# Four graph layers on one core: a written order for the first pass of the last layer, and its adjacency kept as fp8

## The chip, the cores and the metric

The kernel runs on one core of one Trainium2 chip. The time is the device time of one execution in microseconds (us). A core has the engines PE (TensorE: matmuls and transposes into PSUM), ACT (ScalarE), DVE (VectorE), POOL (GpSimd) and SP (SyncE, used here only to issue DMAs). Each engine runs its own list of instructions in order and waits at an instruction whose inputs, or whose output buffer, are not there yet. ACT and POOL issue DMAs as well, from the same list as their computing.

## The reference

Sixteen graphs (B) of 1024 nodes (N) with 128 features (D). `adj` is a 0/1 matrix for each graph. Four layers follow one another, each as `x = layernorm(x + layer(x))`:

- layer 0: attention masked by `adj`
- layer 1: for each node the maximum over its neighbours of `relu(p_i + q_j + b)`
- layer 2: sum over neighbours, then a two-layer perceptron
- layer 3: first a pruned adjacency, made row by row ("dilation": every so many neighbours of a row are removed, together with the mirrored entry, so that later rows see what earlier rows removed), then three SAGE steps with a batch norm over all graphs after each:

```python
def _sage(x, adj, Wr, Wx, b, mf):
    deg = jnp.clip(jnp.sum(adj, axis=-1, keepdims=True), 1.0, None)
    agg = jnp.einsum('bij,bjd->bid', adj, x) / deg
    out = agg @ Wr + x @ Wx + b
    nrm = jnp.maximum(jnp.linalg.norm(out, axis=-1, keepdims=True), NORM_EPS)
    return out / nrm * mf[..., None]

adj_d = _dilate(adj, mask)
h1 = _bn(jax.nn.relu(_sage(x, adj_d, Wr1, Wx1, b1, mf)), g1, be1)
h2 = _bn(jax.nn.relu(_sage(h1, adj_d, Wr2, Wx2, b2, mf)), g2, be2)
h3 = _bn(jax.nn.relu(_sage(h2, adj_d, Wr3, Wx3, b3, mf)), g3, be3)
xc = jnp.concatenate([h1, h2, h3], axis=-1) * mf[..., None]
return (xc @ Wl + bl) * mf[..., None]
```

A batch norm needs all sixteen graphs, so layer 3 falls into passes over the graphs. The dilation needs only `adj`, not the features.

## The kernel before, in words

**Main loop (`layers_012`).** `slot(s, last)` (L853) is one step of layer 1's maximum; 86 slots make a graph (`NP`), 1376 the loop. Beside each slot a planner lets streams advance: `scores` and `attend` of the next graph (layer 0), `rest` of the graph before (layer 2), and `dilation()`, which handles 32 rows (R) of all graphs at a time and writes what is removed to `removed` in DRAM (`removed<-gone`, L611). The planner's costs and due times fix the order, and the loop stands inside `tc.manual_schedule`, which keeps PE, ACT, DVE and POOL in the order of the program. `load_columns(at)` (L749) loads chunk `at` (120 rows, 9 chunks to a graph) of the transposed adjacency `adjT` from fp32 into the fp8 tile `AT`, by a POOL DMA that casts. `AT` has four buffers.

**After the loop.** The last graph's `rest` (L402: relu of the maximum, layer norm, sum over neighbours `pa`, perceptron `pp` and `py`, layer norm) is written out next, and then `first_edges()` (L1124), which loads layer 3's weights through ACT's DMA queue (`weight`, L112) and calls `edges(0)`, `settle(0)` and `edges(1)`. From the end of the loop on, the order on each engine is the scheduler's.

**Edges.** `edges(b)` (L967) makes the pruned adjacency of graph b. `load_edges` (L957) brings in `gone_all` (the removals) and `near` (the transposed adjacency, once more from fp32), both by casting POOL DMAs. For each of 16 half rows of chunks, PE adds the removals and their transpose in PSUM (`pgone`, L973 and L975: five matmuls) and DVE clears the edge in `near` (L977). `near` is stored as `kept`. Then 16 matmuls count the degrees (`pdeg`, L984), ACT copies them, and a DMA to DRAM and one back turn the row of 1024 into 8 rows of 128 (`degree`, `deg_t`). `settle` (L991) takes min, max and reciprocal on DVE and stores `there` and `share` to DRAM; `load_share` (L999) reads `share` back to all 128 partitions.

**First pass (L1145 to L1158), for each graph.** `expanded` (L1004) turns `near` into eight fp32 chunks `m` on ACT. `convolve` (L1011) splits the features into `high` (ACT) and `low` (DVE), sums over neighbours in 32 matmuls (`pagg`, L1021) and multiplies by `share` (`u`, L1024). `sage` (L1027) makes `po` from the features and from `u` (L1032, L1035), `o` on ACT, transposes to `rows`, squares (ACT), sums (DVE), takes the power -1/2 on POOL (L1051) and writes the rows `r_rows` on DVE (L1055). `pass_on` (L1116) transposes back (`phid`, L1063), keeps statistics, stores `hidden`, and runs `convolve` again on the new rows for the second pass (`around`). At the end of graph b the program calls `edges(b + 2)`.

**The rest.** `second(b)` (L1160) and `pass_on` make the second pass, `second` and `columns` the third, `summed` and a layer norm the output. They use the same helpers.

Of the kernel before, what the change touches and what calls it, by code (L numbers as in the profile page):

```python
# [48 lines left out]
R, G = 32, 4  # L49
K, Q = N // R, B // G  # L50
# [23 lines left out]
def tile_graph_layers(ctx: ExitStack, tc, a, out):  # L74
# [6 lines left out]
    small = ctx.enter_context(tc.tile_pool(name="small", bufs=3))  # L81
    psum = None
# [14 lines left out]
    penalty = consts.tile([P, P], BF, name="penalty")  # L97
# [7 lines left out]
    lit = consts.tile([CH, PC, P], F8, name="lit")  # L105
    nc.gpsimd.dma_start(out=lit, in_=a["lit"])
    less = consts.tile([P, P], F32R, name="less")
    nc.vector.tensor_scalar_mul(less, ident, -1.0)
    one_less = consts.tile([P, 1], F32, name="one_less")
    nc.sync.dma_start(out=one_less, in_=a["one_less"])  # L110

    def weight(name, shape=(P, P), how=None, pool=consts):  # L112
        t = pool.tile(list(shape), F32, name="w_" + name)
        src = a[name] if how is None else a[name].rearrange(how[0], **how[1])
        nc.scalar.dma_start(out=t, in_=src)
        return t

    def column(name, n=1, pool=consts):
        return weight(name, (P, n), ("(c p) -> p c", {"p": P}), pool)

    def row(name, pool=consts):
        return weight(name, (1, P), ("(o f) -> o f", {"o": 1}), pool)
# [5 lines left out]
    Wd = consts.tile([P, P], F32, name="Wd")  # L128
# [4 lines left out]
    eps1 = consts.tile([P, 1], F32, name="eps1")  # L133
# [3 lines left out]
    def in_three(v, name):  # L137

        p = bank("p3")
        nc.tensor.matmul(p[:, :P], ones[0:1, :], v, start=True, stop=True)  # L140
        left = temp.tile([3, P], F32, name="left_b")
        nc.vector.tensor_copy(left, p[:3, :P])
        e = consts.tile([3, P], BF, name=name)
        nc.vector.memset(e, 0.0)
        for i in range(3):
            part = temp.tile([3, P], BF, name="part_b")
            nc.vector.tensor_copy(part, left)
            if i < 2:
                nc.vector.tensor_sub(left, left, part)
            nc.vector.scalar_tensor_tensor(e, part, ident[:3, i:i + 1], e, op0=ALU.mult, op1=ALU.add)  # L150
        return e
# [8 lines left out]
    half_mask = consts.tile([B, N], F32, name="half_mask")  # L160
# [7 lines left out]
    half_rows = consts.tile([P, K, Q], F32, name="half_rows")  # L168
# [6 lines left out]
    of_graph = consts.tile([P, G], F32, name="of_graph")  # L175
    nc.vector.tensor_reduce(of_graph, ident.rearrange("p (g r) -> p g r", g=G), axis=mybir.AxisListType.X, op=ALU.add)

    above = consts.tile([P, Q, R], BF, name="above")
    nc.vector.memset(above, 1.0)
    running = consts.tile([P, Q, R], BF, name="running")  # L180
# [5 lines left out]
    of_row = consts.tile([P, R], F32, name="of_row")  # L186
# [6 lines left out]
    removed_T = dram.tile([K, P, Q, N], BF, name="removed_T")  # L193

# [43 lines left out]
    def layers_012():  # L238
# [510 lines left out]
        def load_columns(at):  # L749
            b, c = divmod(at, T + 1)  # L750
            if b < B:
                rows = min(CH, N - c * CH)
                t = AT[at] = apool.tile([CH, N], F8, name="AT", bufs=4)
                if rows < CH:
                    nc.gpsimd.memset(t, 0.0)
                nc.gpsimd.dma_start(out=t[:rows], in_=adjT[b, c * CH:c * CH + rows])
# [96 lines left out]
        def slot(s, last):  # L853
# [11 lines left out]
            if s >= 0 and g % PC == 0:  # L865
                load_columns(b * (T + 1) + g // PC + 2)
# [62 lines left out]
        assert not streams, streams  # L929
        last = rest(B - 1)  # L930
        for _ in range(15):
            next(last)
        for _ in dilate:
            pass
        right.close()
        for _ in last:
            pass
        psums.close()
        psum = ctx.enter_context(tc.tile_pool(name="psum", bufs=2, space=PSUM))
        first_edges()  # L940


# [14 lines left out]
    def load_edges(b):  # L957
        gone = ep.tile([P, T, N], F8, name="gone_all")
        q, g = divmod(b, G)
        rows = removed[:, g * R:(g + 1) * R, q, :].rearrange("(c k) r i -> k r c i", c=T)  # L960
        for k in range(P // R):
            nc.gpsimd.dma_start(out=gone[k * R:(k + 1) * R], in_=rows[k])
        near = ep.tile([P, T, N], F8, name="near", bufs=2)
        nc.gpsimd.dma_start(out=near, in_=adjT[b].rearrange("(c p) i -> p c i", p=P))
        return gone, near

    def edges(b):  # L967

        gone, near = load_edges(b)
        for c in range(T):  # L970
            for h, s in enumerate(halves):
                p = bank("pgone")
                nc.tensor.matmul(p, ident_b, gone[:, c, s], start=True, stop=False)  # L973
                for t in range(4):
                    nc.tensor.matmul(p[:, t * P:(t + 1) * P], gone[:, 4 * h + t, c * P:(c + 1) * P], ident_b,  # L975
                                     start=False, stop=(t == 3))
                nc.vector.tensor_tensor(near[:, c, s], near[:, c, s], p, op=ALU.is_gt, saturate=False)  # L977
        nc.sync.dma_start(out=kept[b], in_=near)

        deg = ep.tile([1, N], F32, name="deg")  # L980
        for s in halves:
            p = bank("pdeg")
            for c in range(T):
                nc.tensor.matmul(p, ones_b, near[:, c, s], start=(c == 0), stop=(c == T - 1))  # L984
            nc.scalar.copy(deg[:, s], p[0:1, :])
        nc.sync.dma_start(out=degree[b], in_=deg)
        d = ep.tile([T, P], F32, name="deg_t", bufs=2)
        nc.sync.dma_start(out=d, in_=degree[b].rearrange("(t i) -> t i", t=T))
        return near, d

    def settle(b, d):  # L991
# [12 lines left out]
    def expanded(near):  # L1004
        m = []
        for c in range(T):
            m.append(sb.tile([P, N], F32R, name="m", bufs=10))
            nc.scalar.copy(m[c], near[:, c, :])  # L1008
        return m

    def convolve(src, m, part):  # L1011

        high = sb.tile([P, T, D], F32R, name="high3")
        nc.scalar.copy(high, src)
        low = sb.tile([P, T, D], F32R, name="low3")
        nc.vector.tensor_sub(low, src, high.bitcast(F32))
        pa = wide("pagg")
        for c in range(T):
            for k, piece in enumerate((high, low)):
                for s in halves:  # L1020
                    nc.tensor.matmul(pa[:, s], piece[:, c, :], m[c][:, s],  # L1021
                                     start=(c == 0 and k == 0), stop=(c == T - 1 and k == 1))
        u = sb.tile([P, N], F32, name="u")
        nc.vector.tensor_mul(u, pa, part)  # L1024
        return u

    def sage(b, u, h, z, weights):  # L1027
# [3 lines left out]
        for s in halves:  # L1031
            nc.tensor.matmul(po[:, s], wx, h[:, s], start=True, stop=False)  # L1032
            if extra is not None:
                nc.tensor.matmul(po[:, s], extra, z[:, s], start=False, stop=False)
            nc.tensor.matmul(po[:, s], wr, u[:, s], start=False, stop=True)  # L1035
        o = sb.tile([P, N], F32, name="o", tag="sq", bufs=2)
        nc.scalar.activation(o, po, AF.Identity, bias=bias)
# [3 lines left out]
        for h in range(2):  # L1041
# [3 lines left out]
            sq = sb.tile([P, 4, D], F32, name="sq_rows")  # L1045
# [6 lines left out]
        nc.gpsimd.tensor_mul(n, n, nm[:, :, b])  # L1052
        for h in range(2):
# [4 lines left out]

    def columns(b, r, stats):
        for h in range(2):  # L1060
            p = bank("phid")
            for t in range(4):
                nc.tensor.transpose(p[:, t * P:(t + 1) * P], r[:, 4 * h + t, :], ident)  # L1063
            nc.scalar.copy(R3[b][:, halves[h]], p)
            nc.vector.bn_stats(out=stats[:, 2 * b + h, :], in_=p)
# [55 lines left out]
    ep, ahead = None, {}  # L1121
    Wr = Wx = bs = gs = bes = Wl = bl = None

    def first_edges():  # L1124
        nonlocal ep, Wr, Wx, bs, gs, bes, Wl, bl
        ep = ctx.enter_context(tc.tile_pool(name="ep", bufs=1, side="right"))
        Wr, Wx, bs, gs, bes = ([f(f"L3_gnn_{w}{l}", pool=ep) for l in (1, 2, 3)] for w, f in (
            ("Wr", weight), ("Wx", weight), ("b", column), ("g", column), ("be", column)))
        Wl = weight("L3_gnn_Wl", (P, 3, P), ("(c p) o -> p c o", {"p": P}), ep)
        bl = column("L3_gnn_bl", pool=ep)  # L1130
        ahead[0] = edges(0)
        settle(0, ahead[0][1])
        ahead[1] = edges(1)

    with ExitStack() as es:
# [6 lines left out]
    nc.vector.tensor_copy(pl, bl)  # L1142
    stats = sb.tile([P, 2 * B, 6], F32, name="stats", bufs=2)
    weights = Wr[0], Wx[0], bs[0], None
    for b in range(B):  # L1145
        x0 = sb.tile([P, T, D], F32, name="h", bufs=2)
        nc.sync.dma_start(out=x0, in_=x3[b])
        part = load_share(b)
        m = expanded(ahead[b][0])
        transposed(R3[b], x0)  # L1150
        r = sage(b, convolve(x0, m, part), R3[b], None, weights)
        if b + 1 < B:
            start = len(nc.cur_bb.bb.instructions)
            settle(b + 1, ahead[b + 1][1])
            behind(nc.cur_bb.bb.instructions[start - 1], start)
        pass_on(b, 0, r, m, part, stats)
        if b + 2 < B:
            ahead[b + 2] = edges(b + 2)  # L1158

    def second(b):  # L1160
# [4 lines left out]
        return sage(b, u, R3[b], z, weights)  # L1165

    weights = batchnorm(0, stats)
    stats = sb.tile([P, 2 * B, 6], F32, name="stats", bufs=2)
    r = second(0)
    for b in range(B):  # L1170
        near = ep.tile([P, T, N], F8, name="near", bufs=2)
        nc.sync.dma_start(out=near, in_=kept[b])
        part = load_share(b)
        following = second(b + 1) if b + 1 < B else None
        pass_on(b, 1, r, expanded(near), part, stats)
# [11 lines left out]
    def summed(b):  # L1187
        hs = []
        for l in range(2):
            r = sb.tile([P, N], F32, name="m", bufs=10)  # L1190
# [11 lines left out]
    for b in range(B):  # L1202
        following = summed(b + 1) if b + 1 < B else None
        xb = sb.tile([P, T, D], F32, name="xb", tag="m", bufs=10)
# [41 lines left out]
```

## Time and profile before

| | |
|---|---|
| median of 3 runs | 6267.28 us (6261.64 to 6274.73) |
| profiled execution | 6289.34 us, its span 6287.6 us |
| mean granted PE clock | 0.951 |
| busy over the span | PE 5624.7 us (89%), DVE 4878.2 (78%), ACT 3981.7 (63%), POOL 3635.9 (58%) |
| main loop, last DVE step | 5002.43 us |
| first pass, PE busy from 5120 to 5780 us | 532.69 of 660 us |
| second pass, PE busy from 5824 to 6040 us | 213.37 of 216 us |
| third pass, PE busy from 6045 to 6166 us | 103.64 of 121 us |
| output, PE busy from 6168 us to the end | 98.12 of 119.6 us |

The page's second part shows each engine in 40 slices of 157 us. A digit is the busy share in tenths; `PEclk` is the clock that the chip granted to PE. An answer by windows gives the same for stretches that one chooses. The chain of waits follows the work that ended last back through what released each step. A busy PE is not PE at its peak: matmuls are pipelined, and the distance from start to start says more than the length of one.

### The profile page before, as it was taken

The numbers are of one execution on the slowest core, as the hardware profiler recorded it, in microseconds if no ns is written. First come the engines' busy times: TensorE is split into PE (matmuls) and PEld (weight loads), VectorE is DVE, ScalarE is ACT, GpSimd is POOL, SyncE is SP. The second block draws the span as 40 slices with busy tenths as digits, with TensorE's granted clock in tenths as the row PEclk, the third lists the DMA queues.
The fourth block names the chain that finished last, engine by engine and source line by source line (L and its number), as shares of the span: only waits on it lengthen the run. The fifth ranks groups of instructions, "written<-read, shape, count | busy, mean of one in ns | idle before, by whom it ended". The sixth has DMA issues, their size and how long they took to land.

```text
span 6287.6 us, 92692 instructions
## 1 busy us (share of the span) xinstructions
PE 5624.7 (89%) x30144; PEld 3091.0 (49%) x30250; DVE 4878.2 (78%) x7402; ACT 3981.7 (63%) x7266; POOL 3635.9 (58%) x11895
## 2 busy tenths in 40 slices
PE   6989999999899989899999999999998678787998
PEld 4545454545454545454444545444543345555654
DVE  3888889898989888888888989888898644444455
ACT  3667676676767676767676767676665533333855
POOL 2676767677767776767776767677776411110113
PEclk8999999999999999999999999999999888898999
DMA  5121212121212121212121212121210246563645
GB/s 39 11 32 21 36 22 36 21 36 22 35 21 36 23 35 21 35 21 35 21 36 21 39 22 35 28 29 29 29 27 11 40 90 128 105 122 106 212 162 187
DMA packets 478410, 317.44 MB, mean 50 GB/s; under 512 B 301162, under 2 KB 429668, under 8 KB 473828
## 3 DMA queue, kind: packets, MB, share of 16 engines
q0 software_dynamic: 105648, 84.20, 15.6%
q1 hardware_dynamic: 367600, 226.13, 12.3%
q8 instruction: 237, 3.88, 0.3%
q10 hardware_dynamic: 4676, 1.19, 0.1%
q14 instruction: 249, 2.04, 0.1%
HBM read 412.71 MB, written 117.18 MB: 84 GB/s over the span
## 4 chain that ended last, share of the span: by engine, by line
PE 31%; DVE 11%; ACT 5%; POOL 4%; issue 2%; DMA 1%; ACTq 0%; SPq 0%; DVEq 0%; POOLq 0%
PE pg L835 7%; PE pagg L1021 6%; DVE best L900 5%; PE pm L804 3%; PE pa L435 1%; PE pav L393 1%; PE pp L296 1%; PE po L1035 1%; ACT hot L805 1%; PE pdeg L984 1%; POOL length L1051 1%; DVE sub L482 1%; PE prank L595 1%; PE psc L345 1%; PE pgone L973 1%
## 5 line engine op out<-in xcount | busy, mean ns | idle before, releaser
L900 DVE TENSOR_TENSOR best<-best,pg 128x1024 f32<-128x1024 f32 x2720 | 3263.5, 1215 | 496.1 <-PE pg L835 484.9
L805 ACT ACTIVATE hot<-pm,one_less 128x512 fp32r<-128x512 f32 x2752 | 1887.2, 689 | 746.7 <-PE pm L804 739.0
L835 PE MATMUL pg<-hot,high 64*128 64x512 f32 x5504 | 1411.2, 509 | 196.0 <-DVE best L900 166.2
L835 PE MATMUL pg<-hot,low 64*128 64x512 f32 x5504 | 1119.7, 404 | 0.0
L804 PE MATMUL pm<-AT,lit 120*128 120x512 fp8e4 x2752 | 1091.2, 397 | 4.0 <-ACT low L826 3.0
L835 PEld LDWEIGHTS pg<-hot,high 64*128 64x128 f32 x5504 | 525.4, 188 | 954.6 <-DVE best L900 440.0
L665 POOL TENSOR_SCALAR sc<-low_counts,half_mask,rest 16x1 f32<-16x1 f32 x992 | 355.9, 359 | 398.5 <-DVE rest L651 287.8
L835 PEld LDWEIGHTS pg<-hot,low 64*128 64x128 f32 x5504 | 540.6, 193 | 0.0
L804 PEld LDWEIGHTS <-lit 120*128 120x128 fp8e4 x2752 | 270.3, 98 | 395.4 <-issue 319.4
L670 POOL TENSOR_SCALAR sc<-sc 16x1 f32<-16x1 f32 x992 | 399.6, 403 | 105.1
L826 ACT CAST low<-pt 128x256 fp32r<-128x256 f32 x688 | 256.1, 372 | 256.6 <-PE pt L824 255.3
L1051 POOL TENSOR_TENSOR length<-length,mhalf 128x8 f32<-128x8 f32 x48 | 78.9, 1644 | 570.1 <-DVE length L1050 570.1
L667 POOL TENSOR_SCALAR sc<-sc 16x1 f32<-16x1 f32 x992 | 322.3, 325 | 107.7
L672 POOL TENSOR_SCALAR hit<-V,sc 16x31 bf16<-16x31 bf16 (+30 forms) x992 | 361.3, 364 | 0.0
L673 POOL TENSOR_SCALAR last_rank<-V,sc 16x31 f32<-16x31 bf16 (+30 forms) x992 | 346.0, 349 | 0.0
L824 PE MATMUL pt<-high,less 128*128 128x256 f32 x688 | 278.8, 405 | 67.7 <-ACT high L819 61.1
L482 DVE TENSOR_TENSOR sub<-sub,q 128x24 f32<-128x24 f32 (+11 forms) x768 | 308.0, 402 | 24.8 <-ACT q L300 10.4
L816 PE MATMUL pt<-ident,sub 128*128 128x128 f32 x1376 | 278.4, 284 | 54.1 <-ACT hot L805 51.8
L1008 ACT CAST m<-near 128x1024 fp32r<-128x1024 fp8e4 x256 | 253.3, 1044 | 113.1 <-DVE near L977 60.0
L393 PE MATMUL pav<-v,eT 128*128 128x128 f32 x2048 | 301.0, 291 | 2.0 <-ACT eT L386 2.0
L393 PEld LDWEIGHTS pav<-v,eT 128*128 128x128 f32 x2048 | 254.9, 196 | 73.0 <-issue 55.3
L666 POOL TENSOR_SCALAR sc<-sc 16x1 f32<-16x1 f32 x992 | 239.4, 241 | 86.5
(271 smaller groups left out, 9828.6 us busy)
## 6 DMA issues: line engine op xcount, KB each, us to landing
removed<-gone SPq DMA_DIRECT2D x128, 256.0 KB
An<-in_adj_dram POOLq DMA_DIRECT2D x16, 1024.0 KB, 14.9
E<-in_adj_dram POOLq DMA_DIRECT2D x128, 128.0 KB, 6.4
gone_all<-removed POOLq DMA_DIRECT2D x64, 256.0 KB, 12.7
near<-in_adjT_dram POOLq DMA_DIRECT2D x16, 1024.0 KB, 17.7
kept<-near SPq DMA_DIRECT2D x16, 1024.0 KB
share<-share SPq DMA_DIRECT2D x32, 512.0 KB
hidden<-r SPq DMA_DIRECT2D x32, 512.0 KB
```

Source lines behind the costliest of these rows:

```text
L393: nc.tensor.matmul(pav, eT[:, c, :], values[b][:, c, :], start=(c == 0), stop=(c == T - 1))
L482: nc.vector.tensor_max(sub[:, :n_g, n:2 * n], sub[:, :n_g, 0:n], qg[:, 2 * g0:2 * g0 + n_g, k:k + 1].to_broadcast([P, n_g, n]))
L665: gp.tensor_scalar(half, mine, half_mask[:, m], rest[:, n:n + 1], op0=ALU.mult, op1=ALU.add)
L667: gp.tensor_scalar(sf, half, 5.5, sf, op0=ALU.is_gt, op1=ALU.mult)
L670: gp.tensor_scalar(to, at, sf, none, op0=ALU.subtract, op1=ALU.subtract)
L672: gp.tensor_scalar(hit[:, n, n + 1:], V[:, n, n + 1:], at, None, op0=ALU.is_equal)
L673: gp.tensor_scalar(last[:, n + 1:], V[:, n, n + 1:], to, None, op0=ALU.is_le)
L804: nc.tensor.matmul(pm, lit[:, r, :], AT[b * (T + 1) + c][:, halves[h]], start=True, stop=True)
L805: nc.scalar.activation(hots[s][:, halves[h]], pm, AF.Relu, bias=one_less)
L835: nc.tensor.matmul(pg[:, a], part[rows, at * P:(at + 1) * P], hots[s][rows, halves[h]], start=(k == 0), stop=(k == 1))
L900: nc.vector.tensor_max(own, own, pg)
L1021: nc.tensor.matmul(pa[:, s], piece[:, c, :], m[c][:, s], start=(c == 0 and k == 0), stop=(c == T - 1 and k == 1))
```

## The change

Six things change together.

1. **fp8 copy.** During the main loop, every `AT` chunk is also stored by SP to `adj8` in DRAM, when the chunk after it is loaded. `load_near` reads `adj8` through SP, without a cast; `load_gone` stays with POOL.
2. **After the loop.** What is left of the dilation, the last graph's `rest` and graph 0's edges are one written order inside `manual_schedule`. `go_on(n)` advances `rest` by n steps; between them stand graph 0's removals (two halves together in a two-bank tile), its degrees, its eight `m` chunks and `settle(0)`, and at the end six of graph 1's eight chunks of removals.
3. **Weights.** Layer 3's weights go through SP's queue.
4. **First pass.** `first_pass` is one written order too. `aggregate` calls `beside(i)` after each of its 16 pairs of matmuls. In graph b's first aggregate the last four removal halves of graph b+1 are placed, in the second the first twelve of graph b+2, the `m` chunks, `settle` and the `high` and `low` of graph b+1. `degrees(b + 1)` and graph b+1's transposes stand between the power on POOL and `r_rows`. The batch norm's factors stand beside the last aggregate.
5. **Halves.** `high`, `low`, `u` and `o` are made in halves, `po` takes both Wx parts ahead of both Wr parts, and `sq_rows` has two buffers. This holds for all passes.
6. **Memory.** Constants of layers 0 to 2 move to a pool `early` that is freed with those layers; `m` moves to the pool `ep`.

The diff, cut to its core:

```diff
@@ load_columns
             b, c = divmod(at, T + 1)
+            if at:
+                before, k = divmod(at - 1, T + 1)
+                rows = min(CH, N - k * CH)
+                nc.sync.dma_start(out=adj8[before][k * CH:k * CH + rows], in_=AT[at - 1][:rows])
...
@@ end of layers_012
-        assert not streams, streams
-        last = rest(B - 1)
-        for _ in range(15):
-            next(last)
-        for _ in dilate:
-            pass
-        right.close()
-        for _ in last:
-            pass
-        psums.close()
-        psum = ctx.enter_context(tc.tile_pool(name="psum", bufs=2, space=PSUM))
-        first_edges()
+            assert not streams, streams
+            for _ in dilate:
+                pass
+            right.close()
+            first_weights()
+            nears[0], nears[1] = load_near(0), load_near(1)
+            gones[0] = load_gone(0)
+            last = rest(B - 1)
...
+            def both_halves(b, c):
+                p = psum.tile([P, 2, 512], F32, tag="wide", name="pgone", bufs=2)
+                for h in range(2):
+                    removals(p[:, h], b, c, h)
+                keep(b, nears[b][:, c, :], p.rearrange("p a n -> p (a n)"))
+
+            go_on(27)
+            for c in range(T):
+                both_halves(0, c)
+            go_on(5)
+            nc.sync.dma_start(out=kept[0], in_=nears[0])
+            gones[1] = load_gone(1)
+            go_on(18)
+            p = psum.tile([P, 2, 512], F32, tag="wide", name="pdeg", bufs=2)
+            degrees(0, [p[:, h] for h in range(2)])
+            go_on(12)
+            expanded(0, range(T))
+            go_on(12)
+            settle(0)
+            for _ in last:
+                pass
+            for c in range(6):
+                both_halves(1, c)
...
@@ loads and removals
+    def load_near(b):
+        near = ep.tile([P, T, N], F8, name="near", bufs=2)
+        nc.sync.dma_start(out=near, in_=adj8[b].rearrange("(c p) i -> p c i", p=P))
+        return near
+
+    def load_gone(b):
+        gone = ep.tile([P, T, N], F8, name="gone_all", bufs=GONE)
...
+    def one_half(b, i):
+        c, h = divmod(i, 2)
+        p = bank("pgone")
+        removals(p, b, c, h)
+        keep(b, nears[b][:, c, halves[h]], p)
...
+    def aggregate(split, m, beside=None):
+        pa = wide("pagg")
+        i = 0
+        for h in range(2):
+            for piece in split[h]:
+                for t in range(4):
+                    c = 4 * h + t
+                    for s in halves:
+                        nc.tensor.matmul(pa[:, s], piece[:, t, :], m[c][:, s], start=(i == 0), stop=(i == 15))
+                    if beside:
+                        beside(i)
+                    i += 1
+        return pa
...
@@ sage
+        u = get_u()
+        o = sb.tile([P, N], F32, name="o", tag="sq", bufs=2)
+        for s in halves:
             nc.tensor.matmul(po[:, s], wr, u[:, s], start=False, stop=True)
-        o = sb.tile([P, N], F32, name="o", tag="sq", bufs=2)
-        nc.scalar.activation(o, po, AF.Identity, bias=bias)
+            nc.scalar.activation(o[:, s], po[:, s], AF.Identity, bias=bias)
...
         nc.gpsimd.tensor_mul(n, n, nm[:, :, b])
+        if meanwhile:
+            meanwhile()
...
@@ first pass (inside manual_schedule)
+        for b in range(B):
+            more, later = b + 1 < B, b + 2 < B
+            if b:
+                expanded(b, range(6, T))
+            if later:
+                nears[b + 2] = load_near(b + 2)
+            following = load_rows3(b + 1) if more else None
+
+            def removals_end(i):
+                if more and i < 4:
+                    one_half(b + 1, 12 + i)
+                if more and i == 3:
+                    nc.sync.dma_start(out=kept[b + 1], in_=nears[b + 1])
+                    if later:
+                        gones[b + 2] = load_gone(b + 2)
+
+            pa = aggregate(split, ms[b], removals_end)
+
+            def degrees_and_columns():
+                if more:
+                    degrees(b + 1, [bank("pdeg"), bank("pdeg")])
+                    transposed(R3[b + 1], following)
+
+            r = sage(b, lambda: scale_by(pa, shares[b]), R3[b], None, weights, degrees_and_columns)
+            split = []
+            for h in range(2):
+                high = high_of(r, h)
+                split.append((high, low_of(r, h, high)))
+                back(b, r, h, stats)
+            nc.sync.dma_start(out=hidden[0][b], in_=R3[b])
+            coming = []
+
+            def removals_begin(i):
+                if later and i >= 4:
+                    one_half(b + 2, i - 4)
+                if more:
+                    if i in (0, 1, 8, 9, 10, 11):
+                        expanded(b + 1, [len(ms.get(b + 1, ()))])
+                    if i == 10:
+                        settle(b + 1)
+                    if i in (11, 13):
+                        h = (i - 11) // 2
+                        high = high_of(following, h)
+                        coming.append((high, low_of(following, h, high)))
+                elif i == 12:
+                    after.append(batchnorm(0, stats))
+
+            after = []
+            pa = aggregate(split, ms.pop(b), removals_begin)
+            nc.sync.dma_start(out=around[b], in_=scale_by(pa, shares[b]))
+            if more:
+                shares[b + 1] = load_share(b + 1)
+            split = coming
```

## The prediction

> **What bounds the kernel now.** I read four views in this order: the page's slices, the stages of layer 3 by windows, the chain of waits inside one graph of the first pass, and the waits of that pass. The slices show a long even part (layers 0 to 2, slices 1 to 31) and then four unequal stages.
>
> ```profile
> PE   6989999999899989899999999999998678787998
> PEclk8999999999999999999999999999999888898999
> DMA  5121212121212121212121212121210246563645
> ```
>
> The windows (time; busy us and count of PE, PE weight loads, DVE, ACT, POOL; granted clock; DMA share) put numbers on the stages:
>
> ```profile
> 5064.00:5120.00 56.00, 36.41 (x198) 22.08 (x196) 20.36 (x32) 14.44 (x19) 5.88 (x10) 0.83 0.71 131
> 5120.00:5780.00 660.00, 532.69 (x2746) 348.61 (x2747) 297.99 (x430) 229.96 (x280) 69.82 (x95) 0.88 0.58 113
> 5824.00:6040.00 216.00, 213.37 (x910) 145.13 (x911) 103.72 (x154) 175.67 (x211) 30.27 (x34) 0.99 0.64 224
> ...
> 5303.74:5309.20 5.46, 1.97 (x9) 1.57 (x9) 3.17 (x7) 1.58 (x3) 1.86 (x2) 0.50 0.01 1
> 5309.20:5312.00 2.80, 2.80 (x9) 1.88 (x10) 2.47 (x3) 0.43 (x1) 0.00 (x0) 0.50 0.49 183
> ```
>
> The second pass (5824 to 6040) is TensorE-bound: 213 of 216 us. The first pass is not: no engine is full. Its period is the distance of the `length` pow (L1051) from graph to graph: 5119.72 for graph 0, 5761.18 for graph 14, so 641.46/14 = 45.82 us. The last two lines lie inside one period: after the wait for `r_rows` TensorE works at half clock, 1.97 + 2.80 = 4.8 us of work that full clock does in 2.4.
>
> The chain before graph 0 shows a serial stretch of DMA trips:
>
> ```profile
> 5068.44 3.63 PE pdeg L984 x16
> 5072.69 5.53 DMA degree<-deg
> 5078.24 4.99 DMA deg_t<-degree
> ...
> 5084.72 5.09 DMA share<-deg_t
> 5089.83 5.53 DMA share<-share
> ```
>
> And the timeline of ACT at the end of the main loop shows graph 15's layer 2 kept back by weight DMAs on ACT's queue (relu of `rest`, L405), though its input was ready at 5002.43:
>
> ```profile
> 5010.18 1.06 ACT L405 ACTIVATE p<-p 128x1024 f32<-128x1024 f32 x1 [14.87 <-DMA w_L_gnn_b<-in_L_gnn_b_dram]
> ```
>
> **The change: steady first pass.** No matmul disappears; waits do. TensorE's work for one graph at full clock, from steps in the chain: `pagg` 64 x 0.228 = 14.6; removals 16 halves x (0.23 + 0.22) = 7.2, plus 0.05 for each switch between the two kinds (a mixed `pagg` takes 0.28) = 0.8; `pdeg` 3.47; `po` 8 x 0.43 = 3.4; `ptr` 0.9; `rows` 1.0; `phid` 1.0. Sum 32.4 us. DVE has about 22 (16 `near` of 0.67, `u` and `low` 4 halves each of 0.65, `sq_rows` sums 1.4, `r_rows` 1.3, statistics 1.3, settle 1.4), ACT about 17 (8 `m` of 1.04, 14 half-size copies of 0.6). So TensorE is the floor if the order hides the rest.
>
> I walked the written order with these durations, t = 0 at the first aggregate. Aggregate with 4 removal halves: to 9.3. `po` with Wx runs 1.7 while DVE makes `u`; Wr, `o` in halves, `rows`: to 14.1. Squares, sums, pow, multiply: `r_rows` starts at 17.6; that stretch (pow alone 1.64) is covered by `pdeg` (to 17.5) and `ptr` (to 18.6). `phid` to 19.8, held 0.8 in all by ACT's copies freeing banks. Second aggregate from 20.0 with 12 removal halves: 1.8 + 12 x 0.96 to 33.4. There DVE has 12 x 0.67 + 1.4 + 1.3 = 10.8 against 11.5 of TensorE, and settle plus two `low` come late in it, so banks are short: 0.6 there and 0.6 at the next removals. Period 34.3. I add 0.7 for late transfers: **35.0**, a gain of 14 x 10.8 = 151 us.
>
> Splitting instructions into halves costs 0.13 each (1.225 for 1024, about 0.68 for 512); DVE and ACT have over 10 us free, so nothing. In passes 2 and 3 the same helpers add some 0.5 to DVE and 0.4 to ACT per graph; pass 2 has 13.6 of TensorE over 11.0 of ACT, so nothing either. If that cover were gone: 0.5 x 16 = 8 us. Pass 3 might shorten (7.17 a graph against 6.5 of TensorE, `sq_rows` now double): 0 taken, down to -10.
>
> **Clock.** The row is 0.50 above, 0.88 on average. The Trainium skill, "TensorE: Matmul & The Clock Gate", section "Part 1: The HAM clock gate", says the array drops to half after an idle window of about 3.4 us and returns after as much sustained work. In my walk TensorE never stands for over 0.6 us, so by the rule all runs at full clock, as pass 2 does (0.99): 35.0. Keeping the row's 0.88 would make 32.4 into 36.8, the period 39.4 and the steady gain 90. I take the rule; the row is the upper end.
>
> **DMAs and queues.** Per graph the adjacency leaves POOL (software cast, 1 MB landing in 17.7 us) for SP with fp8 rows of 1 KB. POOL keeps four `gone_all` issues (2.3 us), then the pow, 11 us later: free. One `gone_all` buffer: removals hold it 17 us, the load needs 12.8 from issue, 15.7 from the first of four (5068.58 to 5084.29); 32.7 fits under 34.3. `near` has 21 us to arrive. A rule speaks against: "Perfetto Trace Analysis", "DMA Optimizations", says that transfers under 2 KB carry significant overhead. The price is between 6.15 us (an estimate: 1 MB in "DMA: Bandwidth & Descriptors", "Bandwidth") and the row's 17.7; both are hidden, so 0 by either. The tightest trip is the share: `deg` copied at 18.1, then the measured 5.5 + 5.0, settle due at 29.4; share store 5.1, load 5.5 behind `around` on SP: lands near 42.4, needed at 44. Each us beyond 1.6 lengthens the period; what waits behind it is `u` on DVE, then Wr.
>
> **Prologue.** The 17 weight DMAs move from ACT to SP: relu at 5002.5, 7.7 earlier. On SP they come before `near`: 13.9 us of issue times after 4992 put it at 5007; landing between 6 and 17.7, taken 9: 5016, when `xT2` is done (5016.9). Eight 1024-wide `near` (nearest row: `best` L900, 1.215) take 9.8 against 7.6 for `parts` beside them: aggregation of layer 2 starts 1.5 late, at 5026. 12.5 for `pa`, 3.6 for `pdeg` now on the path, 10 to the sum on DVE, settle waiting 1 for its degrees and taking 1.4, statistics 1.7, POOL 3.7, ACT 3.2: 5063 (before 5062). The degree trips and removals now lie before that; graph 1's `gone_all`, asked for after the eighth `near` (about 5026), lands at 5042 and is first needed at 5055. Load of x 5.5, then transposes and aggregate with a cold start 11, `po` to pow 6.5: pow of graph 0 at about 5088 instead of 5119.7. Gain **31** (21 if `near` needs 17.7).
>
> **Ends.** Graph 14 to 15: 33.7 becomes about 30.7, bound by the degree trips; batchnorm beside the last aggregate: 29.2 becomes about 25. Gain **7**.
>
> **Main loop.** 144 stores of 120 KB on SP, 0.34 issue each, in queue with the removals' transfers. DVE waited for `hit_p` three times, 26 us in all, and DMA is 0.1 to 0.2 busy. Taken 0; bounds -5 (order noise) and +10. In the walk nothing waits for them: an AT buffer is reused three chunks (some 109 us) after its store is issued.
>
> Sum 151 + 31 + 7 = 189. The profiled execution took 6289.34 (span 6287.6 and 1.7 around it), 22 above the median 6267.28; I take the same difference off both: 6100 profiled, **6078** median.
>
> **Rivals.**
> Late trips: SP runs its list in order, so degree and share wait behind each other and `u` stands. With 2 us more on each of four trips: 8 - 1.6, period 41.4, gain 62 + 38: 6167. For: the chain above, and a DMA share of 0.6. Against: those trips were measured beside other loads.
> Order no better than the scheduler's: cold clock and bank waits stay, period 44: gain 25 + 38, 6204. This is also the case that the change doesn't do what it says. Against: pass 2 fills TensorE with the same pieces.
> Slower: in the main loop a store on SP waits for its AT load (landing 3.9, at worst 29.1) and holds `hit` and `hit_p` behind it, for which DVE stands in fixed order. It decides from 189/31 = 6.1 us per block of 32 rows; at 8 it gives 6267 + 248 - 189 = 6326. For: the one place where `hit_p` was late, DVE stood 15.3 us. Against: the stored chunk was issued 36 us earlier, so it has landed.
>
> **How the numbers follow.** Forecast (period 33 to 38.5) 0.73; late trips 0.14; order no better 0.07; slower 0.05; nothing visible 0.01. Low end: period 33, prologue 36, pass 3 10, ends 10: 6267 - 179 - 56 = 6032, rounded to 6030. High end: period 40, prologue 25, ends 5: 6267 - 81 - 30 = 6156, rounded to 6155. A measurement of this kernel can tell about 0.2%, 12.5 us: faster 0.94, same 0.01, slower 0.05.
>
> **What would show it.** Right: pow L1051's successor every 34 to 36 us, PE busy over 90% and clock above 0.96 in the first pass, relu of `rest` within 1 us of the last `total`, no `pdeg` or share trip between graph 15's layer 2 and graph 0's aggregate. Wrong: `u` waiting for `share<-share`, TensorE waiting for `gone_all`, DVE waiting for `deg_t`, or a main loop that ends later than 5002.

## The result, and the profile after

The median of the changed kernel is 6203.88 us (6199.75 to 6207.63, four runs), against 6269.40 us for the kernel before: a ratio of 0.9896 (95% interval 0.9879 to 0.9913). It is faster, by about 65 us instead of the predicted 189. The forecast was 6078 with a range up to 6155, so the time lies 49 us above the range.

The profiled execution took 6199.75 us (span 6198.0). Reading the same marks in both traces, the last DVE step of the main loop and the starts of the `length` pow on POOL (L1051 before, L1116 after), gives the balance. The last column is what the prediction said.

| stage, us | before | after | difference | predicted |
|---|---|---|---|---|
| start to end of main loop | 5002.43 | 5091.19 | **+88.8** | 0 (-5 to +10) |
| loop end to pow of graph 0 | 117.29 | 86.62 | -30.7 | -31 |
| first pass, pow of graph 0 to 14 | 641.46 | 505.39 | -136.1 | -151 |
| graph 14 to 15, and on to the second pass | 62.88 | 51.28 | -11.6 | -7 |
| second pass, to pow of the third | 228.24 | 233.27 | +5.0 | 0 |
| third pass | 108.35 | 102.69 | -5.7 | 0, down to -10 |
| output | 126.95 | 127.56 | +0.6 | 0 |

The differences sum to that of the spans, 6287.6 to 6198.0 or -89.6 (to rounding). One row holds the miss. All that the change meant to do in layer 3 happened nearly to size, and the main loop, where the change adds a store per chunk (and moves constants to another pool), became 89 us longer.

The page's slices of the changed kernel, first row TensorE busy, then its clock, then the DMA share:

```profile
PE   5989899989898989999989798989999878999998
PEclk8999999989999999999999899999999989999999
DMA  5021213121212212122121211212121014554645
```

In the main loop, a 9 of TensorE's row has become an 8 or a 7 in slices 5, 9, 13, 21, 23, 25 and 27, and the clock loses a tenth in slices 9 and 23 (slices are 155 us wide here and 157 before, so single digits also shift: slice 17 went up). The whole loop by windows, before and then after, in the columns of the next table:

```profile
0.00:5002.43 5002.43, 4570.86 (x25280) 2434.43 (x25386) 4301.27 (x6339) 3411.56 (x6488) 3432.54 (x11536) 0.96 0.21 28
0.00:5091.19 5091.19, 4566.92 (x25280) 2433.90 (x25386) 4292.97 (x6339) 3410.36 (x6488) 3422.65 (x11535) 0.96 0.22 31
```

Every engine is busy for as long as before, to within 10 us, and the mean clock is the same, so the 89 us are waiting and not slower work. The first pass, slices 35 to 37, now reads 9, 9, 9 where it read 7, 8, 7.

The windows of the changed kernel (time; busy us and count of PE, weight loads, DVE, ACT, POOL; granted clock; DMA share; GB/s): one graph of the first pass, twelve graphs, the second pass, the third pass.

```profile
5213.91:5250.01 36.10, 34.17 (x194) 21.15 (x193) 20.61 (x34) 15.41 (x22) 4.23 (x6) 1.00 0.52 148
5213.91:5647.11 433.20, 410.01 (x2306) 253.81 (x2305) 247.32 (x408) 184.98 (x264) 50.84 (x72) 1.00 0.53 147
...
5743.61:5937.23 193.62, 193.62 (x815) 127.64 (x814) 92.58 (x154) 170.43 (x225) 25.79 (x29) 1.00 0.64 224
5977.63:6070.44 92.81, 92.61 (x366) 45.78 (x366) 55.09 (x99) 47.94 (x84) 25.80 (x29) 1.00 0.23 72
```

A graph takes 36.10 us, TensorE is busy for 410.01 of 433.20 us (95%) and the clock is 1.00 throughout. The third pass, whose PE was busy for 103.64 of 121 us, has no gap left from its second graph on.

The loop's gaps are found in its waits. SP is not one of the engines kept in program order, and its own waits in the main loop are now these (SPq is SP's list of DMA issues; line, what it waits for: us in all, times, longest):

```profile
SPq L758 <- DMA AT<-in_adjT_dram: 2846.5, 138, 54.8
SPq L686 <- POOL hit L678: 463.6, 24, 29.7
SPq L615 <- DVE gone L613: 372.7, 47, 19.4
```

L758 is the new store. At 138 of 144 stores SP stands, 20.6 us on average, because the chunk to be stored has not been *loaded* yet. A load takes 3.9 us from issue to landing (the median), so on average SP is there well before the load is even issued. What this does to others is in the loop's waits for DMAs:

```profile
DVE gone L613 <- DMA removed<-gone: 80.6, 9, 18.0
...
PE ptr L290 <- DMA X<-in_x_dram: 38.2, 5, 20.3
...
DVE hit_T L703 <- DMA hit_p<-hit: 23.6, 2, 14.4
```

In the loop of the kernel before the first does not exist, and the other two were:

```profile
PE ptr L286 <- DMA X<-in_x_dram: 9.8, 1, 9.8
DVE hit_T L699 <- DMA hit_p<-hit: 26.0, 3, 15.3
```

One place shows the chain link by link. First the timeline of SP, then a line of POOL's and one of DVE's:

```profile
611.68 34.12 SPq L758 DMA_DIRECT2D adj<-AT  x2
645.85 0.58 SPq L615 DMA_DIRECT2D removed<-gone  x1
646.52 0.41 SPq L622 DMA_DIRECT2D removed_T<-last_T  x1
```

```profile
642.28 0.65 POOL L764 DMA_DIRECT2D AT<-in_adjT_dram  x1 [0.29 <-POOL AT L763]
```

```profile
648.55 0.55 DVE L613 TENSOR_SCALAR gone<-rank,least,match 128x1024 bf16<-128x1024 f16 x1 [18.03 <-DMA removed<-gone]
```

The first row holds two stores: SP issued one at 611.68 and then stood at the next until 645.8. POOL asked for that next store's chunk only at 642.28. Meanwhile the `removed<-gone` transfers waited behind the store on SP; their source buffers stayed occupied, and DVE stood 18.03 us before it could write the next `gone`. DVE runs in fixed order, so the loop's `best` stood with it.

### The profile page after: what moved, and what is told of

It is laid out like the page before. It is cut to its first block, busy times and chain, and to the rows that moved or that the text cites. A ratio compares the mean times of both kernels' runs of the same rounds, so it can differ in the third digit from the quotient of the medians.

```text
span 6198.0 us, 93287 instructions
## 1 busy us (share of the span) xinstructions
PE 5582.7 (90%) x30144; PEld 3046.0 (49%) x30250; DVE 4870.0 (79%) x7484; ACT 3988.2 (64%) x7362; POOL 3613.1 (58%) x11879
## 3 DMA queue, kind: packets, MB, share of 16 engines
q0 software_dynamic: 89008, 67.42, 12.6%
HBM read 362.38 MB, written 133.96 MB: 80 GB/s over the span
## 4 chain that ended last, share of the span: by engine, by line
PE 31%; DVE 10%; ACT 4%; POOL 3%; issue 2%; DMA 1%; SPq 0%; DVEq 0%; POOLq 0%; ACTq 0%
PE pg L843 7%; PE pagg L1071 5%; DVE best L908 5%; PE pm L812 3%; PE po L1101 2%; PE po L1095 1%; PE pa L439 1%; PE pav L397 1%; PE pp L300 1%; ACT hot L813 1%; PE pdeg L1026 1%; DVE near L1014 1%; PE psc L349 1%; PE prank L599 1%; PE pe L387 1%
## 5 line engine op out<-in xcount | busy, mean ns | idle before, releaser
L1116 POOL TENSOR_TENSOR length<-length,mhalf 128x8 f32<-128x8 f32 x48 | 78.9, 1644 | 489.2 <-DVE length L1115 489.2
L349 PE MATMUL psc<-kT,qT 128*128 128x256 f32 x1024 | 276.3, 388 | 9.9 <-issue 9.9
```

The source lines that it names most:

```text
L349: nc.tensor.matmul(psc[:, 256 * i:256 * (i + 1)], qT[:, t * P:(t + 1) * P], kT[:, s.start + 256 * i:s.start + 256 * (i + 1)], start=False, ...
```

## The experiments

Theories at the start. **Queue:** SP stands at stores whose chunk is not there, and holds back the transfers behind it whose data are ready. **Traffic:** some 17 MB more to write (the pages have 133.96 MB against 117.18) slow other transfers of the loop. **Placement:** the added statements, buffers and pool changes alter the order of the loop on the four fixed engines or their memory. All runs of a group share their runs of the kernel before (median 6276.36 us for the first four, 6275.39 for the next four, 6277.88 for the last).

**e1: no copy.** The stores are left out, and `near` comes from fp32 again:

```diff
-                nc.sync.dma_start(out=adj8[before][k * CH:k * CH + rows], in_=AT[at - 1][:rows])
...
-        nc.sync.dma_start(out=near, in_=adj8[b].rearrange("(c p) i -> p c i", p=P))
+        nc.gpsimd.dma_start(out=near, in_=adjT[b].rearrange("(c p) i -> p c i", p=P))
```

> The changed kernel without the fp8 copy: no stores of AT chunks in the main loop, and near comes from the fp32 matrix by a casting DMA on POOL as before. Queue theory (SP stands at each store for its AT load and keeps the removals' and features' transfers behind it): the last DVE step of the main loop goes from 5091 back to about 5002, total about 6204 - 89 = 6115, up to 6150 if near now comes late for the removals in the first pass. Rival, placement of constants or tiles (the pool named early): the stores are not the cause, the loop still ends near 5091 and the total stays near 6204. Traffic theory (18 MB of more writes slow other transfers down) expects the same as the queue theory here.

Measured: 6178.43 us, 0.9838 (0.9820 to 0.9856). The loop ends at 4992.3, so the loss comes with the stores. But the first pass is slower: 41.2 us a graph instead of 36.1, and 103.7 us instead of 86.6 ahead of it. The wait that replaced the copy's benefit, in e1's first pass, and a piece of its chain:

```profile
DVE u L1075 <- DMA share<-share: 120.9, 13, 9.7
```

```profile
5325.09 12.10 DMA share<-share
```

With the cast, `near` lands 21.2 us after its issue (the median), and the share's trip takes 11.3 to 12.1 us from graph to graph, where it took 5.53 in the kernel before. e1 changes the cast, the bytes read (fp32 has four times those of fp8) and the queue together, so it does not say which of them makes the trips long. By these stages the fp8 copy is worth 14 x 5.1 = 72 us in the first pass and 17 in the prologue, about as much as its stores cost in the main loop.

**e2: the store on POOL.** The same store, behind the loads in POOL's list, which is in program order:

```diff
-                nc.sync.dma_start(out=adj8[before][k * CH:k * CH + rows], in_=AT[at - 1][:rows])
+                nc.gpsimd.dma_start(out=adj8[before][k * CH:k * CH + rows], in_=AT[at - 1][:rows])
```

> The changed kernel with the AT stores issued by POOL instead of SP, at the same place of the program; the same bytes move. Queue theory: SP's list is as before the change, the loop ends at 5002 to 5012 (144 issues of about 0.65 us on POOL, which is some 68% busy), total 6115 to 6125. Traffic theory: the bytes are the cause, the loop still ends near 5091, total about 6204.

Measured: 6103.49 us, 0.9729 (0.9715 to 0.9744). The loop ends at 5013.9 in an execution that took 15 us more than e2's median; the waits for `removed<-gone` are gone, `X` is waited for once (10.0 us, as in the kernel before), and 36.10 us a graph stay. The same bytes at the same points of the program cost little or nothing: the traffic theory falls.

**e3: the kernel before, with the stores alone.** Nothing reads what they write.

> The kernel before with the AT stores on SP added and nothing else (nobody reads the copy). Queue and traffic theories: the whole loss is in this one part, the loop ends near 5091 and the total is about 6268 + 89 = 6357, at least 6340. Placement theory: the total stays near 6268.

Measured: 6378.16 us, 1.0165 (1.0150 to 1.0180), 102 us slower than the kernel before. Its loop ends at 5084.2, 81.7 us later than before, with nearly the same row on SP, and layer 3 is as before (45.8 us a graph):

```profile
SPq L755 <- DMA AT<-in_adjT_dram: 2839.5, 140, 55.0
```

Without any other part of the change the stores bring the loss, to within the scatter of the loop's end (see e7): the placement theory falls.

**e4: SP in program order.** The changed kernel, with SP in a fixed order too for as long as the main loop lasts:

```diff
-            for s in range(-2, B * NP):
-                slot(s, B * NP)
+            with tc.manual_schedule(engines={mybir.EngineType.SP}):
+                for s in range(-2, B * NP):
+                    slot(s, B * NP)
```

> The changed kernel with SP too kept in the order of the program within the main loop (same instructions, same queue, same bytes; only SP's list is in another order). Queue theory: in program order a store stands 36 us behind its load and ahead of nothing that is ready, SP's wait at the stores (2846 us) all but goes, the loop ends near 5002, total about 6115, up to 6140 if the program's order keeps some other transfer back. Traffic theory: about 6204.

Measured: 6099.36 us, 0.9717 (0.9703 to 0.9731). The loop ends at 5002.0 and the pow of graph 0 starts at 5089.02 (the prediction: 5088). SP now waits for what is computed, and seldom for a chunk:

```profile
SPq L615 <- DVE gone L613: 1846.5, 120, 54.0
SPq L686 <- POOL hit L678: 977.2, 24, 50.7
...
SPq L758 <- DMA AT<-in_adjT_dram: 160.6, 26, 31.2
```

SP still stands for thousands of us, as it did in the kernel before (1954.4 us for `gone` alone), and that costs nothing: it stands for the work that is due next. What counts is not how long a queue waits but what is ready behind the waiting instruction. From the pow of graph 0 to the end, e4 takes 1014.2 us and the changed kernel 1020.2; the medians are 104.5 apart. Less those 6.0 us, the stores' place on SP costs some 98 us by the medians, and 89 by the loop's end in the two profiles.

**e8: the kernel before, with SP in program order and no stores**, to see whether the order brings something by itself.

> The kernel before with only SP put into program order in the main loop; no stores. If SP's order cost only what the stores brought, no change: 6276 within 0.3%, loop end near 5002. If the scheduler's order on SP already held transfers back in the kernel before, or program order is itself better, the loop gets shorter: the waits of DVE for hit_p were 26 us in all, so down to 6250. If program order holds loads back, slower.

Measured: 6283.71 us, 1.0006 (0.9995 to 1.0017), loop end 4998.1: no difference that these runs can tell. In the kernel before SP's list was harmless; the order repairs what the stores broke.

**e9: the store later in the program.** Can the loss be cured without a fixed order? SP's list is the scheduler's again, and each chunk is stored when the second chunk after it is loaded:

```diff
-            if at:
-                before, k = divmod(at - 1, T + 1)
+            for old in ([at - 2] if b < B else [at - 2, at - 1]):
+                if old >= 0:
+                    before, k = divmod(old, T + 1)
```

> The changed kernel, SP's list left to the scheduler, but each AT chunk is stored one chunk later in the program (when the second chunk after it is loaded, some 36 us later). If the scheduler puts a store on SP by its place in the program less a fixed lead of some 30 us, the load has landed by then: SP no longer stands at the stores, the main loop ends near 5002 and the time is about 6100, as with SP in program order. If it puts the store on SP as soon as, in its own reckoning of time, the data are there, whatever the program says, SP stands as before, the loop ends near 5091 and the time stays at 6204. In between if only the lead on some chunks exceeds the extra 36 us.

Measured: 6208.51 us, 0.9891 (0.9874 to 0.9907); the loop ends at 5100.5. SP stands as in the changed kernel:

```profile
SPq L759 <- DMA AT<-in_adjT_dram: 2851.6, 139, 55.2
```

One chunk (36 us) later in the program changed next to nothing in how long SP stands at the stores. This speaks for the reading that the scheduler puts the store where its data are there by its own reckoning of time; that reckoning itself is in no trace, so this much stays inference. That distance in the program is no protection on a queue outside the fixed order is shown.

**e5: the cover taken away.** On e4; graph b+1's degrees and transposes leave the gap between the pow and `r_rows`:

```diff
-        if meanwhile:
-            meanwhile()
...
-            r = sage(b, lambda: scale_by(pa, shares[b]), R3[b], None, weights, degrees_and_columns)
+            r = sage(b, lambda: scale_by(pa, shares[b]), R3[b], None, weights)
...
+            degrees_and_columns()
```

> The kernel with SP in program order, but in the first pass graph b+1's degrees and transposes (pdeg and ptr, 4.4 us of TensorE) stand after graph b's phid instead of in the gap between the pow on POOL and r_rows. If they are the cover of the pow chain, as the prediction's walk has it, TensorE stands some 3.5 to 4 us a graph there: a period of 36.1 + 4 = 40 us instead of 36.1, and 44 if the degree and share trips, now 2 us later, make u wait or the idle time takes the clock down. If the order inside the gap does not matter, 36 to 37.

Measured, one run: 6191.98 us, 43.05 us a graph. TensorE now waits in each graph for `r_rows`, and after it works at half clock. From TensorE's timeline, and the windows around it:

```profile
5159.76 1.71 PE L1128 MATMUL phid<-ident,r_rows 128*128 128x128 f32 x8 [4.37 <-DVE r_rows L1121]
```

```profile
5160.00:5162.00 2.00, 1.49 (x9) 1.05 (x8) 1.76 (x4) 1.80 (x4) 0.00 (x0) 0.55 0.00 0
5162.00:5164.00 2.00, 2.00 (x6) 0.73 (x6) 1.12 (x2) 0.20 (x1) 0.00 (x0) 0.60 0.47 197
5164.00:5166.00 2.00, 2.00 (x12) 0.88 (x9) 0.00 (x0) 0.57 (x1) 0.00 (x0) 1.00 0.20 74
```

Of the 7.0 us more than in e4, TensorE stands for 4.8 us (6.7 a graph against 1.9) and is busy 2.2 us longer for the same work (36.3 against 34.2); the longer work goes with the clock, 0.55 to 0.60 for about 4 us after the gap. No wait of `u` for the share appears, so the higher end of what was expected came by the clock and not by late trips. This is the mechanism that the prediction set its steady pass on, seen from the other side: the 4.4 us of `pdeg` and `ptr` hide the pow chain and keep the clock at 1.00.

**e6: one buffer for `sq_rows`**, on e4.

```diff
-            sq = sb.tile([P, 4, D], F32, name="sq_rows", bufs=2)
+            sq = sb.tile([P, 4, D], F32, name="sq_rows", bufs=1)
```

> The kernel with SP in program order, sq_rows with one buffer instead of two. If the second buffer made the third pass shorter (7.17 to 6.63 us a graph), it goes back to about 7.2 and the third pass to about 108 us; if the halves of o did it, it stays at 6.6. In the first pass the second Square then waits for the first sum (0.7 us on a chain with pdeg and ptr as cover): period 36.1 to 36.8.

Measured, one run: 6094.50 us. The third pass (15 distances of the pow) takes 106.6 us against 99.3 in e4, but 2.3 us of the difference lie in the first distance (8.83 against 6.50), which reads 9.88 in the changed kernel with two buffers and so is not the buffer's. From the second distance on a graph takes 6.98 us, against 6.63 in e4 and 7.17 in the kernel before. So the second buffer brings 0.35 of the 0.54 us; what brings the rest, the halves of `o` or something else, was not tested. The first pass stays at 36.1. The total says nothing here: in this run the loop ended at 4978.6, 23 us earlier than in e4.

**e7: two more edits**, on e4. In the first pass the halves of `po` are two tiles, and `near` of graph 0 is asked for ahead of the weights:

```diff
-        po = wide("po")
+        if meanwhile:
+            pos = [bank("po"), bank("po")]
+        else:
+            po = wide("po")
+            pos = [po[:, s] for s in halves]
...
-            first_weights()
-            nears[0], nears[1] = load_near(0), load_near(1)
+            open_ep()
+            nears[0] = load_near(0)
+            first_weights()
+            nears[1] = load_near(1)
```

> The kernel with SP in program order, and two more edits. In the first pass the halves of po are two tiles of one bank each, so that Wr on the second half does not wait for o of the first (0.8 us a graph in the trace): period 36.1 to about 35.3, 12 us in all. And near of graph 0 is asked for ahead of the 17 weights on SP, which is 16 us of issue time earlier, where DVE waited 12.8 us for near: 5 to 6 us of the prologue. Together about 17 us below 6099, so 6082. If the wait for o is only a label on a delay of something else, the period stays at 36.1 and 6 us remain, 6093; if banks get scarce for phid and the removals, the period rises.

Measured: 6064.13 us, 0.9665 (0.9649 to 0.9681), the fastest of all. Two waits had pointed to it. In the changed kernel's first pass this was TensorE's largest wait (us in all, times, longest), and in its prologue DVE stood for the first `near`:

```profile
PE po L1101 <- ACT o L1102: 10.9, 14, 0.8
```

```profile
5109.42 1.22 DVE L1014 TENSOR_TENSOR near<-near,pgone 128x1024 fp8e4<-128x1024 fp8e4 x1 [12.84 <-DMA near<-adj]
```

The first wait is gone in e7 and the period is 35.06 us; its window of one graph:

```profile
5134.00:5169.06 35.06, 34.04 (x194) 21.14 (x193) 20.59 (x35) 15.40 (x23) 4.23 (x6) 1.00 0.56 151
```

The prologue is 5.1 us shorter than in e4 (81.9 against 87.0), as expected. Steady pass 14.6, prologue 5.1 and graph 14 to 15 2.0 make 21.7 us. The medians are 35.2 apart (their runs of before, 6276.36 and 6275.39, agree). The other 13.5 us are not explained; in the profiles it is the main loop that differs, whose program the two kernels share. The loop ended between 4976.1 and 5002.0 in the profiled executions of e4 to e7, so a difference of this size between single executions carries no meaning. Longer executions have the lower mean clock (of e8's twelve, 6258.11 us at 0.957 and 6287.02 at 0.951); why the clock differs is open.

## Why the prediction was right and wrong, point by point

**Main loop: the step that failed.** "Taken 0; bounds -5 (order noise) and +10", and "in the walk nothing waits for them". The walk used the program's place of each store. On SP the program's place does not hold: the fixed order covers PE, ACT, DVE and POOL alone, and SP's list was the scheduler's. The term that was put at 0 measured 88.8 us, 2.8 us for each of the 32 blocks of rows: SP stood 2846.5 us at the stores and kept back transfers that were ready. e3 shows the loss without the rest of the change, e2 and e4 take it away with the stores still there. One of the signs of being wrong that the prediction named, a main loop that ends later than 5002, is what happened.

**A number hit by luck.** "Order no better than the scheduler's" was put at 6204, and the median is 6203.88. Its mechanism did not happen: the period is 36.1 and not 44, and the clock of the first pass is 1.00. The time is the sum of a gain near the forecast and a loss elsewhere.

**The slower rival had the mechanism, and the argument against it was wrong.** "Against: the stored chunk was issued 36 us earlier, so it has landed." In the place shown SP reached the store before POOL had even issued the load. Nor was the argument quite true in program order: e4 still has 26 such waits, up to 31.2 us, but no wait for `removed<-gone` follows from them and its loop ends at 5002.0. What was held was also another thing than named: not `hit` and `hit_p` (26.0 us before, 23.6 after) but `removed`, whose source buffer DVE needs again, and the load of `X`, which TensorE needs. The price, 2.8 us a block, stayed under the rival's point of decision of 6.1, so the sign of the forecast held.

**First pass: right in kind, the walk 1.8 us a graph too short.** 35.0 was predicted, 36.1 measured, TensorE at 95% and the clock at 1.00. e5 shows that `pdeg` and `ptr` are the cover. But 35.0 was a walk of 34.3 and 0.7 for late transfers, and no transfer is late: the first pass has no wait for a DMA. So that 0.7 hid a part of the walk's error by luck. (The walk's own last steps, 33.4 and twice 0.6, add up to 34.6.) Some 1.1 us of the error lie between the start of Wr and the end of `rows`, 3.1 us in the walk and 4.2 in the trace: the walk let Wr run on the second half of `po` straight after the first; it waits for `o` of the first half (0.8 us in the row shown with e7 and in the stretch below, 1.04 by the difference of e7). The rest is spread over steps that are each a little longer than their estimate. The stretch in the trace:

```profile
5244.01 1.02 PE L1101 MATMUL po<-u,w_L_gnn_Wr 128*128 128x512 f32 x2
5245.81 1.12 PE L1101 MATMUL po<-u,w_L_gnn_Wr 128*128 128x512 f32 x2 [0.78 <-ACT o L1102]
5246.77 0.60 PE L1109 MATMUL rows<-ident,o 128*128 128x128 f32 x4
5247.71 0.66 PE L1109 MATMUL rows<-ident,o 128*128 128x128 f32 x4 [0.34 <-ACT o L1102]
5248.20 2.11 PE L1026 MATMUL pdeg<-near,ones_b 128*128 128x512 fp8e4 x9
```

Between the clock rule of the Trainium skill ("TensorE: Matmul & The Clock Gate", "Part 1: The HAM clock gate") and the 0.88 of the row before, the rule was the right choice: with no wait of TensorE above 0.8 us the clock is 1.00, and in e5 one gap of 4.4 us a graph brings 0.55 back.

**The fp8 copy: "both are hidden, so 0 by either" was wrong.** For `near` the prediction allowed 6.15 to 17.7 us and called both harmless. e1 has the cast at 21.2 us, and the share then takes up to 12.10 us: 41.2 us a graph. The late trips rival had put its period at 41.4, with `u` waiting for the share as here; that the numbers agree is chance, since it had 2 us more on each of four trips by SP's order, and in e1 the share, issued right behind `around` as in the changed kernel, is itself longer. The rule of the Trainium skill against transfers under 2 KB ("Perfetto Trace Analysis", "DMA Optimizations") was outweighed here: issued at 5103.82, the 1 MB in rows of 1 KB was used by DVE at 5109.42, so the trip took 5.6 us at most, where the casting load of the kernel before took 17.7. What longer rows would have taken was not measured.

**Prologue: right as a sum, in part by luck.** -30.7 for -31. `near` was issued 12.6 us after the end of the loop and not about 5 us after it, since SP began the 17 weights 3.9 us before the end of the loop and not 10; its trip was 5.6 and not 9. So it was there some 4 us later than in the walk, and e7, which asks for it first, takes 5.1 us off; the other steps must have been shorter by about as much. The relu of `rest` started at 5091.23, 0.04 us after the last DVE step, as foreseen.

**Ends and later passes.** -11.6 for -7. Third pass -5.7, inside "down to -10", and for the larger part by the second `sq_rows` buffer, as named (e6). The second pass was not 0: a graph takes 13.80 us in every kernel with the change and 13.60 before, 2.3 us in all. TensorE is full in both, and the halves make it change between kinds of matmul more often; that this is the 0.2 us was not tested. The step from the second pass to the third moves between executions (27.77 before, 30.52 after, 26.89 in e4), and why is open.

**The median.** The prediction took the 22 us by which the profiled execution of before lay above its median off the result. The changed kernel's profiled execution lay 4 below its own, so 26 of the 126 us between 6078 and 6203.88 are this difference and not the change; by profiled times the miss is 6199.75 - 6100 = 99.8, and the loop is 88.8 of it.

## What to carry to other kernels

Ask of each queue who decides its order before asking what it waits for: on an engine outside the fixed order, "issued long before in the program" proves nothing, and one transfer that waits for its source holds every ready transfer behind it. A store that is off the path belongs on a queue whose order is fixed, behind the load that it depends on (e2), or its queue is put in order too (e4). When a part of a change loses as much as it brings, as the fp8 copy did, look for the place of the loss first: here taking the part out gave 25 us, and giving it another place gave 100.

## What the runs showed of the hardware that was not expected

- 1 MB of fp8 in rows of 1 KB arrived within 5.6 us of its issue on SP's queue; the same 1024 x 1024 matrix by the casting DMA from fp32 took 17.7 us in the kernel before and 21.2 us in e1 (medians), and there the 512 KB broadcast of the share beside it took 11.3 to 12.1 us, against 5.53 in the kernel before.
- Wr on the second half of `po` waited 0.8 us for ACT's copy of the first half, which lies in the other bank of the same PSUM tile; with a tile for each bank (e7) the wait was gone and the period 1.04 us shorter. Whether the chip or the program's tracking of whole tiles keeps the two apart is not shown.
- The profiled loop end of the same loop code moved by 26 us between executions (4976.1 to 5002.0), so the loop could not be judged on single runs below that size.
